# An attention block on one core: the residual x gets the projection's bias ahead of time and waits in DRAM

## The chip, the core and the metric

The kernel runs on one core of one Trainium2 chip. A core has five engines that run side by side, each through its own list of instructions in order, and wait for each other by semaphores: TensorE (PE) multiplies matrices into the accumulators (PSUM), VectorE (DVE) and ScalarE (ACT) read the accumulators and work elementwise, GpSimd (POOL) works elementwise on the on-chip memory (SBUF), and SyncE (SP) issues the DMA transfers to and from DRAM. The metric is the device time of one execution in microseconds (us), lower is better.

## The reference

A group norm, eight heads of self-attention over 2304 positions, an output projection with its bias, and the input added back; B = 4 batches, C = 512 channels, 48 x 48 positions.

```python
hn = _group_norm(x, gn_scale, gn_bias)
qkv = jnp.einsum('oc,bchw->bohw', qkv_w, hn) + qkv_b[None, :, None, None]
qkv = qkv.reshape(b, 3, num_heads, d, t).astype(jnp.float16)
q, k, v = (qkv[:, 0], qkv[:, 1], qkv[:, 2])
w = jnp.einsum('bhct,bhcs->bhts', q * scale, k * scale)
w = jax.nn.softmax(w, axis=-1)
a = jnp.einsum('bhts,bhcs->bhct', w, v).astype(jnp.float32)
out = jnp.einsum('oc,bchw->bohw', proj_w, a) + proj_b[None, :, None, None]
return x + out
```

What the change touches is the last line and the bias before it: `x + proj_b`, to which the product of the projection is added.

## The kernel before

**Tiling.** The 512 channels are four chunks of 128 partitions (`NC = 4`); the 2304 positions are five blocks (`QBLOCKS`): four of 512 columns and one of 256 (`NQ = 5`). The eight heads are four pairs per batch, so there are 16 pairs (`NG`), and of each pair 27 *bursts* (`stream`, 432 in all). The main loop (line 1544) runs over the bursts `n`. In each burst `scores` puts six matmuls into three accumulators and ACT takes their exponentials (`p`, line 1099), `add` sums the exponentials of the block on DVE (`acc`, line 1148), and `values` multiplies those of two bursts earlier by v (line 1117). After the last burst of a block come, a burst apart each: the sums (`sl`, copied to `slx`, line 1192, and sent by SP, line 1195), their reciprocal on DVE (line 1224, stored as `row` by line 1226), the reading back of the row spread over partitions (`ib`, line 1236) and the division on POOL (`att`, line 1244).

**The work beside the bursts.** Everything else that PE has to do is cut into *pieces* in the list `beside`: the chains of q and k (line 821), of v (line 873) and of the projection (line 979). `fill` gives each burst one chain, as a credit allows. All these chains use the one accumulator `pw` (`ps_w`, one buffer), so a chain can start only when DVE has emptied it of the chain before: lines 832 (`q`, `k`), 881 (`v`) and 1003 (`r`). DVE works in order, so this emptying comes behind whatever DVE has been given before it.

**The projection.** Of each batch there are 18 chains of eight matmuls (`proj_list`): for each of the four large blocks one chain for each chunk of 128 output channels, and two for the small block, of two chunks each. They run in the next batch's time: those of batches 0, 1 and 2 stand at about 630 to 760, 1040 to 1160 and 1450 to 1545 us, those of batch 3 in the last 50 us. Before a block's chains `att32` casts the heads' results to `a` on ACT (line 971) and POOL (line 969). `residual` loads the chain's part of x into a tile `r` (line 924), `add_bias` adds the bias `bproj` to it on POOL, chunk by chunk (line 935), `evacuate` adds the product from the accumulator to it on DVE (line 1003), and `store` sends it to the output (line 1006). There are `RES = NC + 2 = 6` buffers `res` for r, and `LEAD = RES - 2 = 4` loads are made ahead when block 0 begins. From then on chain k, once emptied, puts its store and the load of chain k + 4 on the list `loads`, which SP issues in the next burst. The buffers `res` also hold the four parts of the projection's weight at the start (`load_wproj`) and one block of x of batch 1 (`SPARE`).

In these same stretches the next batch is brought in: SP loads its x (line 521) when PE has done with the old block, DVE takes its statistics (line 643) and normalizes it (line 775), with one reciprocal root on POOL in between (`rstd`, line 666, which DVE takes up in line 676).

**The weight's split.** Each part of the weight is split by `split_wproj` into `whi` and `wlo` (DVE, lines 574 to 578), and POOL tests that nothing is left over (lines 579 and 580); `test_split` takes the minimum of that test on DVE (line 583). In the list `beside` it stands between the chain of k and the chain of q.

```python
for j in range(NQ):
    if j < NC:
        put_run(load_wproj, j)
    if j > 0:
        put_run(split_wproj, j - 1)
    put_qk(g + 1, 1, (j,))
    if j > 0:
        put_run(test_split, j - 1)
    put_qk(g + 1, 0, (j,))
```

Of the kernel before, what the change touches and what calls it, by code (L numbers as in the profile page):

```python
# [12 lines left out]
F32 = mybir.dt.float32  # L13
# [4 lines left out]
ALU = mybir.AluOpType  # L18
# [457 lines left out]
def fast_path(  # L476
# [11 lines left out]
):  # L488
    nc = tc.nc

    RES = NC + 2
    LEAD = RES - 2
    const = ctx.enter_context(tc.tile_pool(name="const", bufs=1))
    xpool = ctx.enter_context(tc.tile_pool(name="xpool", bufs=1))
    qkp = ctx.enter_context(tc.tile_pool(name="qkp", bufs=3))
# [281 lines left out]
    def piece(us, run, first=False, last=False, when=None):  # L777
        return [us, run, first, last, when, 0, NG]
# [129 lines left out]
    def rows_of(dram_tensor, b, j, chunks):  # L908
        o, n = QBLOCKS[j]
        found = dram_tensor[b, chunks[0] * P : (chunks[-1] + 1) * P, o : o + n]  # L910
        return found.rearrange("(m p) n -> p m n", p=P)

    def residual(b, j, chunks):
        n = QBLOCKS[j][1]
        if in_two(b, j):

            tag = f"x{chunks[0]}_{(j - NQ + 2) % 3}"
            xt = xpool.tile([P, QB], F32, tag=tag, name=f"r_{b}_{j}_{chunks[0]}")
        else:
            xt = work.tile(  # L920
                [P, QB], F32, tag="res", bufs=RES, name=f"r_{b}_{j}_{chunks[0]}"
            )
        xt = xt.rearrange("p (m n) -> p m n", n=n)
        nc.sync.dma_start(xt, rows_of(x, b, j, chunks))
        res[b, j, chunks[0]] = xt
        unbiased.append((now[0] + 2, (b, j, chunks[0]), chunks))

    unbiased = deque()

    def add_bias():  # L930
        _, key, chunks = unbiased.popleft()
        xt = res[key]
        for i, m in enumerate(chunks):
            bias = bproj[:, m : m + 1].to_broadcast((P, xt.shape[2]))
            nc.gpsimd.tensor_tensor(xt[:, i], xt[:, i], bias, ALU.add)  # L935

    def in_two(b, j):

# [50 lines left out]
    def proj_run(b, j, chunks, pairs=range(NC), bank=None):  # L989

        n = QBLOCKS[j][1]
        if bank is None:
            bank = chain_bank(f"pr_{b}_{j}_{chunks[0]}")
        places = [bank[:, i * n : (i + 1) * n] for i in range(len(chunks))]
        xt = res[b, j, chunks[0]]
        while any(k == (b, j, chunks[0]) for _, k, _ in unbiased):
            add_bias()
        for m, ps in zip(chunks, places):
            proj_chain(b, j, m, ps, pairs)

        def evacuate():
            ps = bank[:, : len(chunks) * n].rearrange("p (m n) -> p m n", n=n)
            nc.vector.scalar_tensor_tensor(xt, ps, DOWN, xt, ALU.mult, ALU.add)  # L1003

        def store(engine=nc.sync):
            engine.dma_start(rows_of(out, b, j, chunks), xt)

        return evacuate, store

    def proj_piece(b, j, chunks, pairs=range(NC), ahead=None):  # L1010
        def run():
            evacuate, store = proj_run(b, j, chunks, pairs)
            evacuate()
            if pairs == LAST:
                finished.add((j, chunks[0]))

            if pairs != FIRST:
                loads.append((now[0] + 1, store))
            if ahead is not None:
                loads.append((now[0] + 1, ahead))  # L1020

        return piece(QB / 290.0 * len(pairs) / NC, run, True, True)

    def proj_pieces(b, j):

# [277 lines left out]
    def put_qk(g, part, blocks=range(NQ)):  # L1303

        for j in blocks:
            put(qk_chain(g, part, j), (g - 2) * per_pair - 1, g)
# [39 lines left out]
    for b in range(B):  # L1346
        g = b * NPAIR
        old = b - 1
        if b == 0:
# [3 lines that stand above are left out]
                if j > 0:  # L1353
                    put_run(split_wproj, j - 1)
                put_qk(g + 1, 1, (j,))
                if j > 0:
                    put_run(test_split, j - 1)
                put_qk(g + 1, 0, (j,))
            for block in SPARE:
                put_run(reload, *block)  # L1360
        put_qk(g + 2, 1)
        put_qk(g + 2, 0)

        late = [j for j in range(NQ) if (b + 1, j) in SPARE]
        early = [j for j in range(NQ) if j not in late]
        tiles = {j: range(o // P, (o + n) // P, 2) for j, (o, n) in enumerate(QBLOCKS)}
        for j in early:
            put_v(b, 1, tiles[j])
        if b == B - 1:
            put_qk(g + 3, 1)  # L1370
            put_qk(g + 3, 0, range(NQ - 1))
            put_convert(old, 0)
            put_qk(g + 3, 0, (NQ - 1,))

            THIRD = range(len(EARLY), NC - 1)
            ahead = [
                (residual, b, j, chunks)
                for j in (NQ - 2, NQ - 3, NQ - 1)
                for jj, chunks in proj_list
                if jj == j  # L1380
            ]
            ahead += [
                (att32, b, j, (c,)) for j in (NQ - 2, NQ - 3, NQ - 1) for c in EARLY
            ]
            ahead.append((att32, b, NQ - 2, THIRD))
            for j in range(NQ):
                put_proj(old, j, ahead)
                if j + 1 < NQ:
                    put_convert(old, j + 1)
            assert not ahead  # L1390

            ahead = [
                (att32, b, NQ - 3, THIRD),
                (att32, b, NQ - 1, THIRD),
                *((att32, b, 0, (c,), True) for c in EARLY),
            ]
            for j in (NQ - 2, NQ - 3, NQ - 1):
                put_first(b, j, ahead if j != NQ - 2 else [])
            put_convert(b, 0)
            put_proj(b, 0)  # L1400
            put_convert(b, 1)
            put_proj(b, 1)
            put_convert(b, NQ - 3)
            put_proj(b, NQ - 3)
            continue

        for j in early:
            if j == NQ - 1 and b > 0:
                put_convert(old, 0)
            put_qk(g + 3, 1, (j,))  # L1410
            put_qk(g + 3, 0, (j,))
            put_run(reload, b + 1, j)
        for j in late:
            put_v(b, 1, tiles[j])
            put_qk(g + 3, 1, (j,))
            put_qk(g + 3, 0, (j,))
        if b > 0:
            for j in range(NQ - 1):
                put_proj(old, j)
                put_convert(old, j + 1)  # L1420
        put_v(b + 1, 0)
        if b > 0:
            put_proj(old, NQ - 1)
        put_qk(g + 4, 1)
        put_qk(g + 4, 0)
        put_qk(g + 5, 1)
        put_qk(g + 5, 0)
# [116 lines left out]
    for n in range(end):  # L1544
        now[0] = n
        idle_once("sync", "scalar", "gpsimd")
        summed = block_at(n - BEHIND - 1)
        if not summed:
            load_due(n)
        wanted(stream[n][0])  # L1550
        inside = n - BEHIND == soon[1]
        scores(stream[n], (lambda: values(stream[n - BEHIND])) if inside else None)
        if summed:

            rows(*summed, add_up(*summed))
            load_due(n)
        if inside:
            expect_end(kinds.DVE)
        while unbiased and unbiased[0][0] <= n:
            add_bias()  # L1560
        if n > 0:
            add(stream[n - 1])
        filled = summed or n - BEHIND - 1 in soon
        if filled:

            fill(n)
        if n >= BEHIND and not inside:
            values(stream[n - BEHIND])
        if block_at(n - BEHIND - 2):
            check_sums(*block_at(n - BEHIND - 2))  # L1570
            invert(*block_at(n - BEHIND - 2))
        if block_at(n - BEHIND - 3):
            spread(*block_at(n - BEHIND - 3))
        if block_at(n - BEHIND - 4):

            divide(*block_at(n - BEHIND - 4))
        if not filled:
            fill(n)
        while joins:
            joins.popleft()()  # L1580
        if n - BEHIND in soon:
            g, j = stream[n - BEHIND][:2]
            sx = rows(g, j, add_up(g, j))
            if n - BEHIND == soon[1]:
                divide_here(g, j, sx, avx[g, j], nc.gpsimd)
        if n - BEHIND - 1 == soon[0]:
            check_sums(g, j)
            invert(g, j)
        if n - BEHIND - 2 == soon[0]:
            spread(g, j)  # L1590
            divide(g, j)
# [143 lines left out]
```

## Time and profile before

| what | value |
|---|---|
| time of three runs | 1602.44, 1603.31, 1604.80 us (median 1603.31) |
| time of the profiled execution | 1603.71 us |
| span of its instructions | 1602.0 us |
| TensorE clock granted, mean | 0.997 |
| DMA | 82.11 MB, 51 GB/s over the span |

The span runs from the first instruction to the last; 1.7 us of the profiled execution's time lie around it. The profile's page gives the busy time of each engine; its views give who waited for whom, the instructions in order of time (start, duration, engine, line, what is written from what, how many, and in brackets the idle time of the engine before it and what ended it), and busy times by stretches of time. A matmul's end is modelled, so that the share of a busy PE tells nothing of its pace; its idle times tell where it waited.

### The profile page before, as it was taken

What the parts mean: (1) busy time and instruction counts of PE and PEld (TensorE: products, weight loads), DVE (VectorE), ACT (ScalarE), POOL (GpSimd) and SP (SyncE); (2) the same over time, 40 slices, a digit from 0 to 9 for tenths busy, and PEclk for the clock granted to TensorE, in tenths of its full rate; (3) what the DMA queues carried; (4) which work ended last, traced back from release to release, by engine and by line L of the source; (5) the groups of instructions that cost most, each with busy time, mean ns of one, the idle gap of its engine ahead of it and who ended that gap; (6) DMA issues with size and microseconds to landing.
All of it is one profiled execution on the core that took longest, in us unless ns stands there. A gap on an engine that the chain in (4) does not pass through costs nothing. (4 is left out here: it accounts for less than half of the span.)

```text
span 1602.0 us, 28595 instructions
## 1 busy us (share of the span) xinstructions
PE 1575.6 (98%) x11526; PEld 679.2 (42%) x11526; DVE 1156.8 (72%) x1302; ACT 1269.6 (79%) x1363; POOL 344.5 (22%) x305
## 2 busy tenths in 40 slices
PE   9999999999999999999999999999999999999997
PEld 3733434443333533445333354344533334434443
DVE  6277668866666678896666666898767666768786
ACT  4177777888888888788888888887878888888885
POOL 1031101101011012621101020253101110027834
PEclk9999999999999999999999999999999999999999
DMA  7002020000000024511000001352000000015423
GB/s 224 1 14 67 12 66 22 18 14 11 14 17 13 11 70 128 147 54 28 11 15 18 14 12 41 118 159 78 19 20 18 15 15 11 15 44 170 131 74 121
DMA packets 94897, 82.11 MB, mean 51 GB/s; under 512 B 50852, under 2 KB 60964, under 8 KB 94756
## 3 DMA queue, kind: packets, MB, share of 16 engines
q1 hardware_dynamic: 92724, 78.35, 17.2%
q8 instruction: 92, 1.51, 0.4%
q10 hardware_dynamic: 1904, 1.84, 0.4%
q14 instruction: 49, 0.40, 0.1%
q0 software_dynamic: 128, 0.01, 0.0%
HBM read 60.70 MB, written 19.17 MB: 50 GB/s over the span
## 5 line engine op out<-in xcount | busy, mean ns | idle before, releaser
L1099 ACT ACTIVATE p<-ps 128x1024 f16<-128x1024 f32 x1296 | 1233.2, 1025 | 301.1 <-PE ps L1092 294.1
L1148 DVE TENSOR_TENSOR acc<-acc,p 128x3072 f16<-128x3072 f16 x270 | 492.1, 1823 | 49.6 <-ACT p L1099 46.8
L821 PE MATMUL pqk<-x,wqkv 128*64 128x512 f32 (+1 forms) x2432 | 510.4, 549 | 0.7 <-DVE k L832 0.6
L1117 PE MATMUL av<-p,v 128*64 128x512 f16 (+1 forms) x2880 | 360.7, 364 | 0.9 <-DVE slx L1192 0.9
L1244 POOL TENSOR_TENSOR att<-avx,ib 128x512 f16<-128x512 f32 (+1 forms) x78 | 132.3, 1696 | 1050.0 <-DMA ib<-row 949.9
L1092 PE MATMUL ps<-q,k 64*128 64x512 f16 (+1 forms) x2880 | 356.0, 358 | 0.5 <-DVE v L881 0.2
L873 PE MATMUL pv<-wqkv,x 128*64 128x256 f32 x2304 | 267.5, 379 | 0.2 <-DVE v L881 0.2
L821 PEld LDWEIGHTS pqk<-x,wqkv 128*64 128x64 f32 x2432 | 168.7, 137 | 206.2 <-issue 155.8
L1092 PEld LDWEIGHTS <-k 64*128 64x128 f16 x2880 | 106.5, 94 | 287.6 <-issue 238.4
L1117 PEld LDWEIGHTS <-v 128*64 128x64 f16 x2880 | 131.3, 109 | 212.7 <-issue 168.0
L873 PEld LDWEIGHTS pv<-wqkv,x 128*64 128x64 f32 x2304 | 166.2, 137 | 81.3 <-DVE v L881 0.6
L1148 DVE TENSOR_TENSOR acc<-p,p 128x3072 f16<-128x3072 f16 x79 | 142.2, 1800 | 0.0
L1153 DVE TENSOR_TENSOR acc<-acc 128x1024 f16<-128x1024 f16 x156 | 120.1, 770 | 3.3
L935 POOL TENSOR_TENSOR r<-r,bproj 128x512 f32<-128x512 f32 (+1 forms) x80 | 105.2, 1336 | 33.0 <-DMA r<-x_dram 16.5
L881 DVE TENSOR_TENSOR v<-pv,bv 128x512 f16<-128x512 f32 x72 | 49.7, 690 | 81.5 <-PE pv L873 81.2
L832 DVE TENSOR_SCALAR q<-pqk,bqkv 128x512 f16<-128x512 f32 (+1 forms) x77 | 53.4, 693 | 74.6 <-PE pqk L821 74.2
L832 DVE TENSOR_SCALAR k<-pqk,bqkv 128x512 f16<-128x512 f32 (+1 forms) x75 | 52.1, 695 | 75.2 <-PE pqk L821 75.0
L979 PE MATMUL pr<-a,whi 128*128 128x512 f32 (+1 forms) x311 | 95.8, 424 | 1.9 <-POOL a L969 1.8
L1192 DVE COPY slx<-sl 128x512 f32<-128x512 f32 (+1 forms) x79 | 50.6, 641 | 62.3 <-PE sl L1176 62.2
L979 PE MATMUL pr<-att,wlo 128*128 128x512 f16 (+1 forms) x311 | 75.8, 364 | 8.8 <-DVE r L1003 8.5
L1003 DVE SCALAR_TENSOR_TENSOR r<-pr,r 128x512 f32<-128x512 f32 x75 | 51.4, 685 | 36.8 <-PE pr L979 13.9
L1126 DVE COPY avx<-av 128x512 f32<-128x512 f32 (+1 forms) x79 | 50.5, 639 | 35.7 <-PE av L1117 35.7
(125 smaller groups left out, 482.6 us busy)
## 6 DMA issues: line engine op xcount, KB each, us to landing
r<-x_dram SPq DMA_DIRECT2D x72, 256.0 KB, 3.7
out_dram<-r SPq DMA_DIRECT2D x69, 256.0 KB, 2.3
ib<-row SPq DMA_DIRECT2D x126, 128.0 KB, 2.9
x<-x_dram SPq DMA_DIRECT2D x62, 256.0 KB, 3.9
x<-x_dram SPq DMA_DIRECT2D x16, 128.0 KB, 5.0
sums<-slx SPq DMA_DIRECT2D x128, 2.0 KB, 2.1
ib<-row SPq DMA_DIRECT2D x30, 64.0 KB, 3.1
wqkv<-qkv_wT_dram SPq DMA_DIRECT2D x2, 768.0 KB, 6.9
```

The costliest lines, as they stand in the source:

```text
L821: nc.tensor.matmul(pw[0][lo : lo + D, :n], wqkv[:, c, w0 + lo : w0 + lo + D], hn[b, c, j], start=(c == 0), stop=(c == NC - 1),)
L832: nc.vector.tensor_scalar(qk[g][part][:, o : o + n], pw[0][:, :n], bqkv[:, col : col + 1], SCALE, ALU.add, ALU.mult,)
L873: nc.tensor.matmul(pw[0][lo : lo + D, a, :], hn[b, c, i * P // QB][:, at + lo : at + lo + D], wqkv[:, c, 2 * C + half * C // 2 :][:, : C / ...
L935: nc.gpsimd.tensor_tensor(xt[:, i], xt[:, i], bias, ALU.add)
L979: nc.tensor.matmul(ps[:, :n], w[:, bass.ts(m, P)], a, start=(i == 0), stop=(i == len(steps) - 1),)
L1003: nc.vector.scalar_tensor_tensor(xt, ps, DOWN, xt, ALU.mult, ALU.add)
L1092: nc.tensor.matmul(ps[:, h, a * n : (a + 1) * n], kt[rows, bass.ts(i, P)], qt[rows, o : o + n], start=True, stop=True,)
L1099: nc.scalar.activation(pt[:, r], ps, AF.Exp)
L1117: nc.tensor.matmul(av[0][lo : lo + D, :n], vv[b, pr // 2][:, i, pr % 2 * P + lo : pr % 2 * P + lo + D], pt[:, r, h, a * n : (a + 1) * n], ...
L1148: nc.vector.tensor_tensor(t, before, pt, ALU.add)
L1153: nc.vector.tensor_tensor(t[:, 0], t[:, 0], t[:, r], ALU.add)
L1244: nc.gpsimd.tensor_tensor(atts[g][:, o : o + n], avx.pop((g, j))[:, :n], ibs.pop((g, j))[:, :n], ALU.mult,)
```

## The change

`residual` no longer loads x but a tile `xb` in DRAM that holds x plus the bias already. These 72 tiles are made by three new steps in earlier bursts: `fetch_x` loads a part of x into a buffer `pre` (two of them; SP), `add_bias` adds the bias two bursts later in one instruction (POOL; before, the small block took two), and `keep_biased` stores it to `xb` a burst after that (SP). `prepare` calls the first and the last at the start of a burst. It makes no fetch before burst 30, none within two bursts of another, none in the bursts in which the `row` or `ib` transfers of a block are due, and none while a chain of the projection is among the next four pieces. The two buffers come from `res`: `RES` is 4 now and `LEAD` is 2, so a residual is loaded when the chain two places before it has been emptied. The wait of a chain for its bias goes. `test_split` stands behind the chain of q now, so one chain later, and for the last part behind the first chain of the next pair.

```diff
-    RES = NC + 2
+    RES = NC
     LEAD = RES - 2
+    FETCH_FROM, FETCH_EVERY = 30, 2
...
-        nc.sync.dma_start(xt, rows_of(x, b, j, chunks))
+        nc.sync.dma_start(xt, biased.pop((b, j, chunks[0])))
         res[b, j, chunks[0]] = xt
-        unbiased.append((now[0] + 2, (b, j, chunks[0]), chunks))
-
-    unbiased = deque()
+
+
+    biased, heavy = {}, set()
+    to_bias = deque((b, j, chunks) for b in range(B) for j, chunks in proj_list)
+    fetched, added = deque(), deque()
+
+    def fetch_x():
+        b, j, chunks = to_bias.popleft()
+        n = QBLOCKS[j][1]
+        name = f"{b}_{j}_{chunks[0]}"
+        t = work.tile([P, QB], F32, tag="pre", bufs=2, name=f"pre_{name}")
+        t = t.rearrange("p (m n) -> p m n", n=n)
+        nc.sync.dma_start(t, rows_of(x, b, j, chunks))
+        fetched.append((now[0] + 2, (b, j, chunks), t))
 
     def add_bias():
-        _, key, chunks = unbiased.popleft()
-        xt = res[key]
-        for i, m in enumerate(chunks):
-            bias = bproj[:, m : m + 1].to_broadcast((P, xt.shape[2]))
-            nc.gpsimd.tensor_tensor(xt[:, i], xt[:, i], bias, ALU.add)
+        _, key, t = fetched.popleft()
+        chunks = key[2]
+        bias = bproj[:, chunks[0] : chunks[-1] + 1].unsqueeze(2)
+        nc.gpsimd.tensor_tensor(t, t, bias.to_broadcast(t.shape), ALU.add)
+        added.append((now[0] + 1, key, t))
+
+    def keep_biased():
+        _, (b, j, chunks), t = added.popleft()
+        name = f"xb_{b}_{j}_{chunks[0]}"
+        kept = dram.tile(list(t.shape), F32, tag=name, bufs=1, name=name)
+        nc.sync.dma_start(kept, t)
+        biased[b, j, chunks[0]] = kept
+
+    fetch_at = [FETCH_FROM]
+
+    def prepare(n):
+        if added and added[0][0] <= n:
+            keep_biased()
+        transfers = block_at(n - BEHIND - 2) or block_at(n - BEHIND - 3)
+        if any(id(p) in heavy for p in beside[:4]):
+            fetch_at[0] = max(fetch_at[0], n + 2)
+        elif to_bias and n >= fetch_at[0] and not transfers:
+            fetch_x()
+            fetch_at[0] = n + FETCH_EVERY
...
-        while any(k == (b, j, chunks[0]) for _, k, _ in unbiased):
-            add_bias()
...
-        return piece(QB / 290.0 * len(pairs) / NC, run, True, True)
+        made = piece(QB / 290.0 * len(pairs) / NC, run, True, True)
+        heavy.add(id(made))
+        return made
...
                 put_qk(g + 1, 1, (j,))
-                if j > 0:
+                put_qk(g + 1, 0, (j,))
+                if 0 < j < NC:
                     put_run(test_split, j - 1)
-                put_qk(g + 1, 0, (j,))
+            put_qk(g + 2, 1, (0,))
+            put_run(test_split, NC - 1)
...
-        put_qk(g + 2, 1)
+        put_qk(g + 2, 1, range(0 if b else 1, NQ))
...
             load_due(n)
+            prepare(n)
...
-        while unbiased and unbiased[0][0] <= n:
+        if fetched and fetched[0][0] <= n and not block_at(n - BEHIND - 4):
             add_bias()
```

On PE and on ACT the order of all instructions stays as it was. Three places show what moves on the others. Names end in a block number, a chunk number and a serial number; the changed kernel's lines from `add_bias` on stand 31 lower than before (1275 is the division of 1244, 667 the root of 666).

**POOL, in the projection of batch 0.** Before, from the division of block 3 of the pair to that of block 4:

```order
L1244 TENSOR_TENSOR att_5605<-avx_3_6405,ib_3_6560 128x512
L935 TENSOR_TENSOR r_2_1_6530<-r_2_1_6530,bproj 128x512
L1217 TENSOR_SCALAR in_4_6655<-sums_170 128x40
L1218 TENSOR_TENSOR tests<-tests,in_4_6655 128x40
L1217 TENSOR_SCALAR in_4_6658<-sums_170 128x40
L1218 TENSOR_TENSOR tests<-tests,in_4_6658 128x40
L935 TENSOR_TENSOR r_2_2_6598<-r_2_2_6598,bproj 128x512
L666 TENSOR_TENSOR rstd<-veps,mhalf 128x2
L935 TENSOR_TENSOR r_2_3_6632<-r_2_3_6632,bproj 128x512
L1244 TENSOR_TENSOR att_5605<-avx_4_6558,ib_4_6703 128x256
```

And the same place in the changed kernel:

```order
L1275 TENSOR_TENSOR att_5765<-avx_3_6586,ib_3_6738 128x512
L1248 TENSOR_SCALAR in_4_6831<-sums_170 128x40
L1249 TENSOR_TENSOR tests<-tests,in_4_6831 128x40
L1248 TENSOR_SCALAR in_4_6834<-sums_170 128x40
L1249 TENSOR_TENSOR tests<-tests,in_4_6834 128x40
L667 TENSOR_TENSOR rstd<-veps,mhalf 128x2
L1275 TENSOR_TENSOR att_5765<-avx_4_6736,ib_4_6878 128x256
```

The three bias additions that stood here are gone; they stand between divisions outside the projections.

**SP, as the projection of batch 1 begins.** Before, from the spread rows of block 4 on:

```order
L1236 DMA ib_4_10439<-row_4_10398 64x256 x2
L1006 DMA out_dram<-r_0_0_10306 128x512
L924 DMA r_1_0_10454<-x_dram 128x512
L1006 DMA out_dram<-r_0_1_10308 128x512
L924 DMA r_1_1_10490<-x_dram 128x512
L1006 DMA out_dram<-r_0_2_10310 128x512
L924 DMA r_1_2_10525<-x_dram 128x512
```

And the same place in the changed kernel:

```order
L1267 DMA ib_4_10741<-row_4_10700 64x256 x2
L1035 DMA out_dram<-r_0_0_10616 128x512
L925 DMA r_0_2_10756<-xb_0_2_4502 128x512
L1035 DMA out_dram<-r_0_1_10618 128x512
L925 DMA r_0_3_10792<-xb_0_3_4534 128x512
L1035 DMA out_dram<-r_0_2_10756 128x512
L925 DMA r_1_0_10827<-xb_1_0_4711 128x512
```

Behind the store of chain 0 the load of chain 2 is issued now, and no longer that of chain 4; it reads `xb`.

**DVE, at the last part of the weight's split** (the burst in which the sums of block 1 are copied to `slx`). Before:

```order
L1126 COPY avx_1_1189<-av_1_1000 128x512
L832 TENSOR_SCALAR k_699<-pqk_1_4_1191,bqkv 128x256
L583 TENSOR_REDUCE tests<-wproj_1043 128x1
L1192 COPY slx_1_1229<-sl_1_1226 128x512
L1148 TENSOR_TENSOR acc_2_1233<-p_2_0_1131,p_2_1_1170 128x3072
```

And the same place in the changed kernel, up to where the test stands now:

```order
L1157 COPY avx_1_1189<-av_1_999 128x512
L833 TENSOR_SCALAR k_699<-pqk_1_4_1191,bqkv 128x256
L1223 COPY slx_1_1228<-sl_1_1225 128x512
L1179 TENSOR_TENSOR acc_2_1232<-p_2_0_1130,p_2_1_1170 128x3072
L833 TENSOR_SCALAR q_698<-pqk_0_4_1234,bqkv 128x256
L1179 TENSOR_TENSOR acc_2_1232<-acc_2_1232,p_2_2_1212 128x3072
L1255 RECIPROCAL inv_1_1282<-sums_168 128x8
L833 TENSOR_SCALAR k_1287<-pqk_1_0_1288,bqkv 128x512
L584 TENSOR_REDUCE tests<-wproj_1043 128x1
```

The test (583, now 584) has moved from ahead of the copy of the sums to six instructions behind it.

## The prediction

> **What bounds the kernel now.** I read the busy times of the page first, then what PE waited for, then the stretches in which it waited.
>
> ```profile
> PE 1575.6 (98%) x11526; PEld 679.2 (42%) x11526; DVE 1156.8 (72%) x1302; ACT 1269.6 (79%) x1363; POOL 344.5 (22%) x305
> PE pr L979 <- DVE r L1003: 8.5, 9, 2.7
> PE pr L979 <- POOL a L969: 1.8, 3, 0.7
> PE av L1117 <- DVE slx L1192: 0.9, 1, 0.9
> PE pqk L821 <- DVE k L832: 0.6, 2, 0.4
> PE count L1674 <- DVE good L1673: 2.5, 1, 2.5
> ```
>
> PE is busy for 1575.6 of 1602.0 us, so all its idle time is 26.4 us. The change gives PE the same instructions in the same order, so it can win only idle time and lost clock. The rows of the waits give total, times and longest. 8.5 us are waits of a projection chain for the emptying of the accumulator, 1.8 for a cast on POOL, 0.9 for the copy of the sums, 0.6 for k; together 11.8. The 2.5 us for `good` belong to the end, which the change does not touch.
>
> ```profile
> 200.00:400.00 200.00, 199.90 (x1556) 85.71 (x1552) 151.06 (x180) 161.27 (x171) 21.88 (x19) 1.00 0.11 26
> 600.00:760.00 160.00, 156.19 (x1178) 74.37 (x1176) 135.24 (x166) 130.72 (x143) 49.19 (x43) 0.99 0.31 90
> 1000.00:1140.00 140.00, 136.67 (x1016) 63.06 (x1014) 122.54 (x154) 115.40 (x129) 53.77 (x45) 1.00 0.35 104
> 1420.00:1560.00 140.00, 136.25 (x882) 61.11 (x880) 108.37 (x106) 120.44 (x136) 79.41 (x64) 1.00 0.39 115
> 673.85:677.25 3.40, 3.40 (x10) 1.78 (x11) 2.30 (x2) 1.07 (x2) 0.18 (x1) 0.54 0.48 151
> ```
>
> These are windows: stretch, length, busy time of PE, weight load, DVE, ACT and POOL, granted clock, DMA share, GB/s. Between projections PE loses 0.1 us in 200. In the three projections it loses 3.8, 3.3 and 3.8; there POOL is two to five times as busy. The last row is the 3.4 us behind the longest wait: the clock is 0.54, which costs 3.4 x 0.46 = 1.6 us more.
>
> **The split test.**
>
> ```profile
> 126.39 0.69 DVE L583 TENSOR_REDUCE tests<-wproj 128x1 f32<-128x512 f32 x1 [1.63 <-POOL wproj L580]
> 127.73 0.84 PE L1117 MATMUL av<-p,v 128*64 128x512 f16 x6 [0.94 <-DVE slx L1192]
> ```
>
> The last test keeps DVE waiting 1.63 us for POOL; behind it stands the copy of the sums, and PE waits 0.94 for that. Moved six instructions back, the test finds its input made. **Gain 0.9**, between 0.2 (the next chain late instead) and 1.2 (with the 0.25 left of the k waits).
>
> **Batch 0.**
>
> ```profile
> 624.77 2.57 DVE L1148 TENSOR_TENSOR acc<-p,p 128x3072 f16<-128x3072 f16 x1
> 628.38 1.95 PE L821 MATMUL pqk<-x,wqkv 128*64 128x256 f32 x16 [0.36 <-DVE k L832]
> 642.81 1.02 PE L979 MATMUL pr<-att,wlo 128*128 128x512 f16 x4 [0.46 <-DVE r L1003]
> 666.48 1.04 POOL L935 TENSOR_TENSOR r<-r,bproj 128x512 f32<-128x512 f32 x1
> 667.48 2.24 POOL L666 TENSOR_TENSOR rstd<-veps,mhalf 128x2 f32<-128x2 f32 x1
> 669.75 1.01 DVE L676 COPY both<-rstd 128x32 f32<-128x32 f32 x1 [0.62 <-POOL rstd L666]
> 673.85 1.86 PE L979 MATMUL pr<-att,wlo 128*128 128x512 f16 x4 [2.68 <-DVE r L1003]
> ```
>
> The longest wait is a chain of queues: a bias addition, behind it on POOL the root `rstd`, behind that on DVE line 676 and the emptying. Without the addition the root starts up to 1.04 us earlier, and DVE has no 0.62 to wait; the normalization behind it runs beside no addition either. I take the 2.68 as gone, with the 1.6 of clock, the 0.36 at 628.38 and a smaller 0.17: **gain 4.8**. The 0.46 at 642.81 stands beside a division and stays. If only 1.04 of the 2.68 goes, and half the clock, it is 2.3; all of it is 5.3.
>
> By the Trainium skill (TensorE: Matmul & The Clock Gate, What's actually happening) the clock falls after at least one idle window of about 3.4 us. This wait was 2.68 and the clock fell right behind it; by the page the 1.6 would not hang on the wait, and the sum would come out 1.6 higher. I go by the row.
>
> **Batch 1.**
>
> ```profile
> 1076.05 2.57 DVE L1148 TENSOR_TENSOR acc<-p,p 128x3072 f16<-128x3072 f16 x1
> 1080.25 1.02 PE L979 MATMUL pr<-att,wlo 128*128 128x512 f16 x4 [0.65 <-DVE r L1003]
> 1084.94 2.44 DVE L775 TENSOR_SCALAR x<-x,ga,gb 128x512 f32<-128x512 f32 x2
> 1088.03 1.02 PE L979 MATMUL pr<-att,wlo 128*128 128x512 f16 x4 [0.88 <-DVE r L1003]
> 1092.89 1.02 PE L979 MATMUL pr<-att,wlo 128*128 128x512 f16 x4 [1.38 <-DVE r L1003]
> 1043.48 0.67 DVE L1003 SCALAR_TENSOR_TENSOR r<-pr,r 128x512 f32<-128x512 f32 x1
> 1046.34 0.42 SPq L924 DMA_DIRECT2D r<-x_dram  x1
> 1050.33 0.68 DVE L1003 SCALAR_TENSOR_TENSOR r<-pr,r 128x512 f32<-128x512 f32 x1
> 1051.43 1.07 POOL L935 TENSOR_TENSOR r<-r,bproj 128x512 f32<-128x512 f32 x1 [1.57 <-DMA r<-x_dram]
> ```
>
> The three waits make 2.91; sums and normalizations stretched beside POOL stand ahead of each. Divisions remain, so I take 2.2 (0 to 2.9). Against it stands the shorter lead: the place after the first store, 1046.34, now loads chain 2, which is emptied at 1050.33. That load, of the same size, was taken up at 1051.43, so chain 2 would be 1.1 late. **Gain 1.1**, between -1.1 and 2.9.
>
> **Batches 2 and 3.**
>
> ```profile
> 1481.41 1.06 PE L979 MATMUL pr<-a,whi 128*128 128x512 f32 x2 [0.54 <-POOL a L969]
> 1487.87 1.02 PE L979 MATMUL pr<-att,wlo 128*128 128x512 f16 x4 [0.43 <-DVE r L1003]
> 1551.85 7.12 POOL L935 TENSOR_TENSOR r<-r,bproj 128x512 f32<-128x512 f32 x4 [9.61 <-DMA r<-x_dram]
> 1553.67 1.02 PE L979 MATMUL pr<-att,wlo 128*128 128x512 f16 x4 [1.41 <-DVE r L1003]
> 1578.44 0.38 PE L979 MATMUL pr<-att,wlo 128*128 128x512 f16 x1 [0.42 <-DVE r L1003]
> ```
>
> In batch 2 the casts stand behind additions on POOL: 1.8 and 0.43, of which I take **2.0** (1.0 to 2.2). In batch 3 the first addition waits for its load and takes a us itself; now two loads are sent instead of four and nothing is added. Of 1.41 + 0.42 I take **1.7** (0.5 to 1.8).
>
> **What the quiet stretches take over.** 72 additions come into them.
>
> ```profile
> 606.28 1.75 DVE L1148 TENSOR_TENSOR acc<-acc,p 128x3072 f16<-128x3072 f16 x1
> L935 POOL TENSOR_TENSOR r<-r,bproj 128x512 f32<-128x512 f32 (+1 forms) x80 | 105.2, 1336 | 33.0 <-DMA r<-x_dram 16.5
> L1244 POOL TENSOR_TENSOR att<-avx,ib 128x512 f16<-128x512 f32 (+1 forms) x78 | 132.3, 1696 | 1050.0 <-DMA ib<-row 949.9
> ```
>
> 105 us of POOL move. In the window 200 to 400, 21.88 us of POOL cost PE at most 0.10; 105 us cost at that rate **0.5**. The other end: a sum beside an addition took 2.57 instead of 1.75, so 0 to 0.82 an addition; at half of it, 0.41, all reaching PE, 72 cost 29.5. I take 0.5, since in that window DVE has a quarter of its time free. What waits newly: each `keep_biased` holds SP until POOL has added, which may stand behind a division; behind it on SP are the sums, rows and spread rows of later blocks, and behind these the divisions. A division waits for its `ib` 949.9/78 = 12 us on the mean already and PE asks for none before the projection: nothing, up to 2 us if that cover fails. The 144 added transfers of 256 KB are 37.7 MB, over some 1000 us 38 GB/s beside 26, which takes the DMA share from 0.11 to about 0.27, below that of the projections: nothing.
>
> The Trainium skill (SBUF — State Buffer, Who interferes with whom) says that a DVE instruction with two SBUF inputs contends with a GpSimd instruction that reads SBUF. The 2.57 agrees; were every addition to hold up a sum for its whole 1.04 us, and PE with it, the sum would be 72 x 1.04 = 75 us worse, which the window speaks against.
>
> **Next late.** With the additions gone DVE is still 85% busy there beside divisions, and some chain is late behind it: **-1.0** (0 to -3).
>
> The sum: 0.9 + 4.8 + 1.1 + 2.0 + 1.7 - 0.5 - 1.0 = 9.0. From the profiled 1603.71 this gives 1594.7; the median is 0.4 lower than that execution, so 1594.3, and I say **1594.5**. All gains at their upper ends make 13.4 (1590), half the sum, 4.5 to 5, 1598.5: its own range. All lower ends together would use the gain up; that they fall together is what the rivals are.
>
> **The rivals.**
>
> *The loads take the wait over.* Loads two places ahead have two bursts: 1043.48 to 1050.33, 6.85 us.
>
> ```profile
> DMA to landing us min/median/max: 2.0/3.0/5.7
> 1562.56 0.69 DVE L1003 SCALAR_TENSOR_TENSOR r<-pr,r 128x512 f32<-128x512 f32 x1 [0.75 <-POOL r L935]
> 1565.08 0.58 SPq L1006 DMA_DIRECT2D out_dram<-r  x1
> ```
>
> The store comes 2.5 us after the emptying where sums are sent ahead of it, the load 0.7 later; with 3.0 to land that is 6.2, still in time, with 5.7 it is 8.9, 2 us late. If 12 of the 72 chains are 0.5 late, 6 us go: 1600.5.
>
> *The bias was not the cause.* Batch 1's three waits stay (2.2 lost) and the next-late term is 3.0 instead of 1.0: gain 4.8, 1598.5. For it: divisions are as many and longer, 1.70 us each. Against it: the longest wait and the casts stand directly behind additions.
>
> *The clock falls anyway*, wait or no wait: 1.6 less gain, 1596.1.
>
> *Slower: the additions stretch DVE in the quiet stretches and PE waits there.* From 9.5/72 = 0.13 us of PE for each addition the gain is used up; at 0.41 it is 1603.7 - 9.5 + 29.5, about 1623. For it: the 2.57. Against it: the window 200 to 400, whose ten-odd us of divisions cost nothing visible.
>
> **How the numbers follow.** Forecast 0.62, loads 0.16, bias not the cause 0.08, clock 0.05, slower 0.09. A measurement of this kernel can tell about 0.2%, 3.2 us, from no change: faster is below 1600.1, slower above 1606.5. Faster: nearly all of the forecast (0.60), the clock (0.05), most of the third (0.06), a third of the loads (0.05), 0.76. Within: the rest of these, 0.14. Slower: 0.10. The range goes from 1589.5, all gains, to 1602, past the loads' 1600.5; what is left out is the slower case and the loads' far end.
>
> **What would show it.** Right: the wait of 2.68 and the 0.54 clock are gone, no PE wait for the copy of the sums near 127, none for the casts, and quiet windows stay above 99.9% PE. Wrong: an emptying that waits for a residual's load (first chain 2 of batch 1), PE idle in quiet stretches behind sums longer than 1.75, or POOL waiting for a `pre` buffer with divisions behind it.

## The result, and the profile after

| what | before | changed |
|---|---|---|
| median of the runs | 1603.59 us (4 runs) | 1592.71 us (4 runs) |
| span of the profiled execution | 1602.0 us | 1591.4 us |
| PE busy | 1575.6 us | 1573.6 us |
| PE idle within the span | 26.4 us | 17.8 us |

The ratio is 0.9933, with a 95% interval of 0.9915 to 0.9950. The forecast was 1594.5, with a range of 1589.5 to 1602. The span is 10.6 us shorter. PE's idle time makes 8.6 of it and its busy time, in which a lower clock shows, 2.0.

First what PE waited for in the changed kernel (total, times, longest, in us), from the view of its waits:

```profile
PE pr L1010 <- DVE r L1032: 1.1, 2, 0.8
PE pv L874 <- DVE v L882: 1.0, 2, 0.9
PE pqk L822 <- DVE v L882: 0.9, 1, 0.9
PE pqk L822 <- DVE k L833: 0.9, 2, 0.6
PE sl L1207 <- DVE avx L1157: 0.8, 2, 0.6
PE first_means L722 <- DVE moments L648: 0.6, 1, 0.6
PE pr L1010 <- POOL a L1000: 0.6, 1, 0.6
```

Of the 8.5 us of waits for an emptied projection accumulator 1.1 are left, of the 1.8 for casts 0.6. Four rows are new or larger: the two of v, k and `avx`, 3.6 us together, against 0.8 before. The wait for `first_means`, at the start of the kernel, was 1.3 before; it lay between under 0.2 and 1.4 in the profiles of this study, also where nothing ahead of it was changed, so its 0.7 us here are no effect of the change.

The same windows of the changed kernel (stretch, length, busy time of PE, weight load, DVE, ACT, POOL, granted clock, DMA share, GB/s):

```profile
200.00:400.00 200.00, 198.17 (x1542) 84.91 (x1540) 157.61 (x179) 159.72 (x169) 46.18 (x35) 1.00 0.24 68
600.00:760.00 160.00, 159.36 (x1212) 75.09 (x1210) 137.23 (x170) 134.54 (x148) 40.59 (x36) 1.00 0.40 121
673.85:677.25 3.40, 3.40 (x21) 1.53 (x20) 3.37 (x5) 3.40 (x6) 2.17 (x3) 1.00 0.61 203
1000.00:1140.00 140.00, 138.76 (x1042) 64.66 (x1038) 121.36 (x154) 117.68 (x130) 28.74 (x29) 1.00 0.42 123
1420.00:1560.00 140.00, 139.10 (x897) 63.54 (x894) 104.62 (x109) 124.48 (x141) 29.20 (x33) 1.00 0.41 121
```

The projections lose 0.6, 1.2 and 0.9 us where they lost 3.8, 3.3 and 3.8, and the clock behind 673 is 1.00. The quiet window 200 to 400 now loses 1.8 instead of 0.1: part of the gain is given back there. Two places of the timeline show how (start, duration, engine, line, operation, what ended the idle time before it):

```profile
273.70 1.04 POOL L946 TENSOR_TENSOR pre<-pre,bproj 128x512 f32<-128x512 f32 x1
273.79 2.57 DVE L1179 TENSOR_TENSOR acc<-p,p 128x3072 f16<-128x3072 f16 x1
277.98 1.94 PE L822 MATMUL pqk<-x,wqkv 128*64 128x512 f32 x8 [0.93 <-DVE v L882]
605.40 1.04 POOL L946 TENSOR_TENSOR pre<-pre,bproj 128x512 f32<-128x512 f32 x1 [2.60 <-DMA pre<-x_dram]
605.49 2.57 DVE L1179 TENSOR_TENSOR acc<-p,p 128x3072 f16<-128x3072 f16 x1
609.37 1.94 PE L822 MATMUL pqk<-x,wqkv 128*64 128x512 f32 x8 [0.64 <-DVE k L833]
```

An addition meets a sum, the sum takes 2.57 instead of 1.75, and the emptying behind it is late for PE. Near 323 the same happens, with 0.87. And the load that comes two places ahead is late once, as batch 1's projection begins:

```profile
1043.68 0.42 SPq L925 DMA_DIRECT2D r<-xb  x1
1048.39 0.69 DVE L1032 SCALAR_TENSOR_TENSOR r<-pr,r 128x512 f32<-128x512 f32 x1 [1.42 <-PE av L1148]
1049.14 1.02 PE L1010 MATMUL pr<-att,wlo 128*128 128x512 f16 x4 [0.80 <-DVE r L1032]
```

The load landed at 1047.93, 4.25 us after its issue, and DVE, which had nothing else to do, empties then. The `av` named in brackets is not what it waited for: the chain to be emptied was complete at 1046.82.

### The profile page after: what moved, and what is told of

Read it like the earlier page. It is cut to its first block, busy times and chain, and to the rows that moved or that the text cites. A ratio compares the mean times of both kernels' runs of the same rounds, so it can differ in the third digit from the quotient of the medians.

```text
span 1591.4 us, 28818 instructions
## 1 busy us (share of the span) xinstructions
PE 1573.6 (99%) x11526; PEld 678.2 (43%) x11526; DVE 1171.2 (74%) x1302; ACT 1269.0 (80%) x1363; POOL 337.0 (21%) x297
## 5 line engine op out<-in xcount | busy, mean ns | idle before, releaser
L1275 POOL TENSOR_TENSOR att<-avx,ib 128x512 f16<-128x512 f32 (+1 forms) x78 | 117.3, 1504 | 1009.0 <-DMA ib<-row 674.7
L1184 DVE TENSOR_TENSOR acc<-acc 128x1024 f16<-128x1024 f16 x156 | 136.4, 874 | 3.3
L946 POOL TENSOR_TENSOR pre<-pre,bproj 128x512 f32<-128x512 f32 x72 | 115.1, 1613 | 22.3 <-DMA pre<-x_dram 21.7
```

The lines of the kernel that those rows point to most:

```text
L946: nc.gpsimd.tensor_tensor(t, t, bias.to_broadcast(t.shape), ALU.add)
L1184: nc.vector.tensor_tensor(t[:, 0], t[:, 0], t[:, r], ALU.add)
L1275: nc.gpsimd.tensor_tensor(atts[g][:, o : o + n], avx.pop((g, j))[:, :n], ibs.pop((g, j))[:, :n], ALU.mult,)
```

## The experiments

The times stand beside runs of the kernel before on the same chip; the experiments ran in three groups, on three chips. The kernel before took 1603.83 beside experiments 1, 2, 3 and 5; 1603.92 beside 6, 7, 9 and the first run of 8; 1603.24 beside 4, 10 and the second run of 8.

**1. No additions at all.** In the kernel before, the three lines that add are left out:

```diff
-        for i, m in enumerate(chunks):
-            bias = bproj[:, m : m + 1].to_broadcast((P, xt.shape[2]))
-            nc.gpsimd.tensor_tensor(xt[:, i], xt[:, i], bias, ALU.add)
```

> The kernel before with the additions of the bias left out (the bias is not added). If PE's waits in the projections come from the additions on POOL (theory): the waits of a projection chain for an emptying or a cast fall from 10.3 us to under 2.5, the clock behind 673 stays at 1.0, about 11 us less, 1592. If they come from DVE's own load and the divisions (rival): under 5 us less, 1598 or more, and the waits of 2.7 and 1.4 stay over 1 us.

Measured: 1589.95 (ratio 0.9908, 0.9893 to 0.9924). A window of this kernel:

```profile
600.00:760.00 160.00, 160.00 (x1216) 75.31 (x1214) 133.79 (x169) 135.43 (x149) 28.33 (x27) 1.00 0.32 91
```

The projection of batch 0 now loses nothing, although all divisions still run there. So the 80 additions cost 13.9 us in their old places. Three waits of 2.4 us together remain before projection chains (1.33, 0.62 and 0.43); the 1.33 stands behind a reciprocal on DVE that waited 2.43 for the transfer of its sums, so not behind a division. The theory stands; the rival falls.

**2. The changed kernel without its additions.** The addition of `add_bias` is left out; fetches and stores to `xb` stay.

```diff
-        bias = bproj[:, chunks[0] : chunks[-1] + 1].unsqueeze(2)
-        nc.gpsimd.tensor_tensor(t, t, bias.to_broadcast(t.shape), ALU.add)
```

> The changed kernel with the additions left out (the bias is not added), all its transfers kept. If the new waits of PE near 278, 323 and 609 us (0.9, 0.9 and 0.6) come from the additions in the quiet stretches (theory): they go, 2.3 us less, 1590.4. If they come from the 144 transfers or from the moved test (rival): they stay, within 0.5 us of the changed kernel.

Measured: 1589.27 (0.9903, 0.9888 to 0.9918), 3.4 under the changed kernel's 1592.71 and 2.4 under the 1591.66 that the same kernel took in experiment 8; each of the three was measured in another group of runs. The window from 130 to 600, in the changed kernel first and then here:

```profile
130.00:600.00 470.00, 468.17 (x3550) 194.26 (x3546) 350.27 (x366) 378.11 (x398) 106.97 (x79) 1.00 0.23 65
```

```profile
130.00:600.00 470.00, 469.89 (x3566) 195.30 (x3564) 335.55 (x369) 379.94 (x400) 50.54 (x46) 1.00 0.23 67
```

The DMA share is the same and PE's 1.8 us of idle time fall to 0.1. The additions make the waits, the transfers none. The late load as batch 1 begins stays, here with a wait of 1.25.

**3. Only the shorter lead.** The kernel before with four buffers, its additions in place.

```diff
-    RES = NC + 2
+    RES = NC
```

> The kernel before with four buffers for the residuals and loads two places ahead; its additions stay in the projections. If the shorter lead costs only the one late load at the start of a batch (theory): 1 to 2 us more, 1604.5 to 1605.5, with a wait of about 2 near 1050 (load plus addition). If the loads as a whole become late (rival): over 6 us more, and waits for the residual in each batch.

Measured: 1619.91 (1.0093, 1.0077 to 1.0108), 16 us more. The theory was wrong by a factor of ten. The rows of PE's and DVE's waits, and the timeline in batch 0:

```profile
PE pr L979 <- DVE r L1003: 26.8, 22, 3.0
DVE r L1003 <- POOL r L935: 40.5, 25, 4.1
...
661.01 0.42 SPq L924 DMA_DIRECT2D r<-x_dram  x1
669.71 0.72 POOL L666 TENSOR_TENSOR rstd<-veps,mhalf 128x2 f32<-128x2 f32 x1 [3.52 <-DVE both L669]
670.40 1.04 POOL L935 TENSOR_TENSOR r<-r,bproj 128x512 f32<-128x512 f32 x1
671.48 0.69 DVE L1003 SCALAR_TENSOR_TENSOR r<-pr,r 128x512 f32<-128x512 f32 x1 [1.76 <-POOL r L935]
672.22 1.02 PE L979 MATMUL pr<-att,wlo 128*128 128x512 f16 x4 [1.77 <-DVE r L1003]
```

DVE's emptyings wait 40.5 us for additions, where they waited 10.5 in the kernel before. In the place shown the load is not late: it landed at 663.93, 2.9 us after its issue. Its addition comes two bursts after the load, which is now just ahead of the emptying, and on POOL it stands behind the root; DVE can empty only when it is done. In other places the addition starts as its load lands. So whether the loads or what stands behind them makes the 16 us was open; experiment 4 settles it.

**4. Only the shorter lead, no additions.** Both edits above together.

> The kernel before with four buffers, loads two places ahead and no additions (the bias is not added). The 16 us of the shorter lead with additions come either from a load that needs an addition behind it before the chain can be emptied (theory): then the shorter lead alone costs 0 to 2 us, 1590 to 1592. Or from the loads landing late (rival): then 1600 and more.

Measured: 1589.23 (0.9911, 0.9896 to 0.9927).

```profile
600.00:760.00 160.00, 160.00 (x1216) 75.25 (x1213) 134.53 (x170) 135.44 (x149) 25.85 (x27) 1.00 0.32 91
```

Without additions the lead of two costs nothing (1589.95 with the lead of four). The load alone is in time, but for the one in the changed kernel as batch 1 begins; a load with an addition behind it is not. So the shorter lead and the earlier bias belong together: the first alone is 16 us slower.

**5. One addition moved.** Of the kernel before, the addition for chain (2, 2) of batch 0 is due a burst later, which puts it behind the root; no other instruction changes its order.

```diff
-        unbiased.append((now[0] + 2, (b, j, chunks[0]), chunks))
+        wait = 3 if (b, j, chunks[0]) == (0, 2, 2) else 2
+        unbiased.append((now[0] + wait, (b, j, chunks[0]), chunks))
```

> The kernel before with one of the 80 additions, the one ahead of the reciprocal root in batch 0, moved behind that root; nothing else. If the longest wait is the queue on POOL and the clock falls because PE stood still (theory): the wait of 2.68 falls under 1.2 and the clock stays at 1.0, 3 to 4.3 us less, about 1599.8. If DVE's load makes it (rival): the wait falls by less than 0.5 us and the time by less than 1. If the clock falls for another reason: the wait is short, the clock at 673 to 677 still about 0.54.

Measured: 1602.4 (0.9992, 0.9983 to 1.0001). The timeline and the clock of the 3.4 us behind the wait:

```profile
666.33 0.72 POOL L666 TENSOR_TENSOR rstd<-veps,mhalf 128x2 f32<-128x2 f32 x1
668.45 1.02 DVE L676 COPY both<-rstd 128x32 f32<-128x32 f32 x1
672.57 1.02 PE L980 MATMUL pr<-att,wlo 128*128 128x512 f16 x4 [1.54 <-DVE r L1004]
679.84 1.02 PE L980 MATMUL pr<-att,wlo 128*128 128x512 f16 x4 [0.62 <-DVE r L1004]
```

```profile
672.57:675.97 3.40, 3.40 (x20) 1.51 (x19) 3.37 (x3) 2.26 (x5) 1.84 (x4) 1.00 0.48 155
```

The wait falls from 2.68 to 1.54, half way between the two theories, and a new one of 0.62 comes behind it. The clock stays at 1.00 behind it. What is left of the wait comes from the steps of DVE between root and emptying, which run beside the moved addition now. The copy of line 676 takes 1.02 here; in the changed kernel, with no addition near, it takes 0.17:

```profile
667.75 0.72 POOL L667 TENSOR_TENSOR rstd<-veps,mhalf 128x2 f32<-128x2 f32 x1 [0.62 <-DVE both L670]
669.95 0.17 DVE L677 COPY both<-rstd 128x32 f32<-128x32 f32 x1
```

So without the queue on POOL 1.1 of the 2.7 are gone, and what is left goes with stretched steps; experiment 7 shows the same from the other side. Here the change wins 0.5 of net idle time and the 1.6 of clock. The times of all runs show 1.4, less than the 3 to 4.3 of the theory, and their interval does not exclude no change.

**6. The move of the test alone,** in the kernel before.

> The kernel before with the move of the test alone. If the wait only changes its place (theory, from the changed kernel's trace): the 0.94 near 128 goes, waits of 0.58 and 0.24 for the copy of av near 103 and 125 come, 0.1 us less. If the move is worth its wait (rival, as predicted): 0.9 us less. The time cannot tell these apart, the waits of PE below 130 us can.

Measured: 1603.34 (0.9998, 0.9988 to 1.0007). Its waits at the two places:

```profile
103.03 0.41 PE L1176 MATMUL sl<-acc,ones 128*64 128x512 f16 x2 [0.58 <-DVE avx L1126]
125.22 0.41 PE L1176 MATMUL sl<-acc,ones 128*64 128x512 f16 x2 [0.24 <-DVE avx L1126]
```

They are the changed kernel's own, to the hundredth. The 0.94 near 128 is gone and 0.82 stand in its place: the test's 0.67 us now stand between q and the next part's split, and the copy of `av` behind them is late. By these waits the move is worth 0.1.

**7. Additions of a tensor and a scalar.** The bias is one number for each partition, so the addition need not read two tensors. In the kernel before (its places kept):

```diff
-            bias = bproj[:, m : m + 1].to_broadcast((P, xt.shape[2]))
-            nc.gpsimd.tensor_tensor(xt[:, i], xt[:, i], bias, ALU.add)
+            nc.gpsimd.tensor_scalar(
+                xt[:, i], xt[:, i], bproj[:, m : m + 1], None, ALU.add
+            )
```

> The kernel before, the additions where they were, but as an operation of a tensor and a scalar of each partition instead of two tensors. If an addition disturbs DVE because it reads two tensors (theory): sums beside it take under 2 us, the waits in the projections fall from 10.3 to under 6, 4 us less or more, 1599. If any POOL work beside DVE disturbs it (rival): waits as before, within 1 us.

Measured: 1605.26 (1.0006, 0.9997 to 1.0015).

```profile
624.54 1.75 DVE L1149 TENSOR_TENSOR acc<-p,p 128x3072 f16<-128x3072 f16 x1
667.58 0.18 DVE L676 COPY both<-rstd 128x32 f32<-128x32 f32 x1 [0.61 <-POOL rstd L666]
670.04 1.02 PE L980 MATMUL pr<-att,wlo 128*128 128x512 f16 x4 [0.64 <-DVE r L1004]
PE pr L980 <- POOL a L970: 5.5, 4, 2.0
PE pr L980 <- DVE r L1004: 5.1, 5, 2.2
```

The sum that took 2.57 beside an addition takes 1.75, and the wait of 2.68 falls to 0.64. The root still stands behind an addition on POOL there, and DVE still waits 0.61 for it; but the copy of line 676 takes 0.18. So of the 2.68 some 0.6 to 1.1 are the queue (this experiment and experiment 5), and the larger part is stretched steps of DVE. But POOL now pays: the addition's mean rises from 1336 to 1867 ns, and casts behind seven and eight of them in a row make PE wait 5.5 us instead of 1.8. The theory stands for the sum, but the waits it wanted under 6 are 10.6, and the time is no better.

**8. The same in the changed kernel,** where no cast stands behind the additions. It ran twice, the second time beside the changed kernel.

> The changed kernel with the additions as tensor and scalar of each partition. By the first theory (two tensors disturb): the waits of 0.9, 0.9 and 0.6 near 278, 323 and 609 shrink, 1 to 2.5 us less than the changed kernel, about 1591. By the rival: 1592.7, the waits stay.

> The changed kernel once more, beside the three others: about 1592.7, with the same new waits near 278, 323, 609 and 1049 us.

> The changed kernel with scalar additions once more. If they help (theory): 1 to 2.5 us under the changed kernel of this call. If the difference of the first time was chance (rival): within 0.7 us of it.

Measured: 1591.13 the first time; the second time 1589.03 (five runs, 1588.68 to 1590.09) beside the changed kernel's 1591.66 (five runs, 1590.49 to 1592.85). The place of before, in the second profile:

```profile
273.38 3.16 POOL L946 TENSOR_SCALAR pre<-pre,bproj 128x512 f32<-128x512 f32 x1
273.44 1.75 DVE L1181 TENSOR_TENSOR acc<-p,p 128x3072 f16<-128x3072 f16 x1
277.22 1.94 PE L822 MATMUL pqk<-x,wqkv 128*64 128x512 f32 x8 [0.52 <-DVE v L882]
```

The addition started first, by 0.06 us, and is still the one that is held up (3.16), where the one of two tensors held up DVE. The wait of 0.93 falls to 0.52, and that of 0.87 goes. The 0.64 near 609 proves nothing: the changed kernel's own second profile does not have it either, since there the addition began 0.87 us ahead of the sum and the sum took 1.78. That profile has the 0.93 and the 0.87 again, and the late load with 0.49. So the theory stands; the gain is 1.6 us across two groups and 2.6 side by side.

**9. Every addition twice.**

```diff
-        nc.gpsimd.tensor_tensor(t, t, bias.to_broadcast(t.shape), ALU.add)
+        for _ in range(2):
+            nc.gpsimd.tensor_tensor(t, t, bias.to_broadcast(t.shape), ALU.add)
```

> The changed kernel with every addition made twice in a row (the bias is counted twice). If a quiet addition costs PE what leaving them out showed (theory, 3.4 us for 72, 0.05 each): 2 to 5 us more, 1595 to 1598. If DVE has little free time left and the next additions all reach PE (rival, 0.41 each): 20 us more or above, 1612.

Measured: 1593.78 (0.9935, 0.9922 to 0.9949), 1.1 over the changed kernel's 1592.71 and 2.1 over its 1591.66, so at the lower edge of the theory or under it, and far from the rival. The longest new wait, of 0.93, grows to 1.77. But DVE is busy 17.7 us longer in the profile and PE idle only 2.0: most of the added time falls where DVE has time to spare. What an addition costs depends more on where it lands than on how many there are.

**10. Scalar additions, and the tests a chain later still.** Behind the next chain of k instead of between q and the next split:

```diff
                 put_qk(g + 1, 1, (j,))
+                if 1 < j:
+                    put_run(test_split, j - 2)
                 put_qk(g + 1, 0, (j,))
-                if 0 < j < NC:
-                    put_run(test_split, j - 1)
```

> The changed kernel with scalar additions, and each test of the split another chain later, behind the next chain of k. If the waits of 0.58 and 0.24 near 103 and 125 come from the test standing between q and the next split (theory): they go, 0.5 to 0.8 us less than with scalar additions alone. If any place there costs the same DVE time (rival): they come back in front of another instruction, no gain.

Measured: 1587.50 (0.9903, 0.9888 to 0.9918; four runs, 1587.37 to 1588.21). Below 130 us one of the waits remains, which all kernels have:

```profile
102.96 1.97 PE L822 MATMUL pqk<-x,wqkv 128*64 128x512 f32 x8 [0.25 <-DVE k L833]
```

The 0.58 and the 0.24 are gone, the 0.94 does not come back. The time is 1.5 under experiment 8's 1589.03, more than the expected 0.5 to 0.8 and than the 0.82 of these waits; the rest has no row of its own. This kernel leaves nothing out and is the fastest of all: 4.2 us under the changed kernel beside it, with no overlap of their runs.

## Why the prediction was right

The time was 1.8 us under the forecast. What gains and what costs was as forecast, with errors in size on both sides that nearly cancel, which is in part luck. Measured by the waits of PE that went and came, in the first profile of the changed kernel:

| term | predicted | measured | from |
|---|---|---|---|
| split test | 0.9 | 0.1 | 0.94 gone, 0.58 and 0.24 come |
| batch 0, with the clock | 4.8 | 5.4 | 0.36, 0.11, 0.46, 0.17, 2.68 gone, clock 1.6 |
| batch 1 | 1.1 | 2.2 | 3.0 gone, late load 0.80 |
| batch 2 | 2.0 | 1.6 | 2.2 gone, one cast late by 0.62 |
| batch 3 | 1.7 | 1.6 | 1.83 gone, 0.28 come |
| quiet additions | -0.5 | -2.3 | 0.93 (0.1 before), 0.87, 0.64 come |
| next late | -1.0 | 0 | the new 0.62 and 0.28 stand with their batches |

The measured rows make 8.6 of the 10.6. A second reading needs no waits: how much earlier the same exponential of ACT (line 1099, now 1130; 1296 of each) starts. It gives:

| stretch, up to exponential | its start in the kernel before, us | gained in the stretch, us |
|---|---|---|
| start, 1 | 73.25 | -0.2 |
| split test, 52 | 137.13 | 0.3 |
| quiet, 456 | 610.61 | -3.0 |
| batch 0, 521 | 692.66 | 5.8 |
| quiet, 821 | 1037.22 | -0.2 |
| batch 1, 881 | 1111.25 | 2.3 |
| quiet, 1181 | 1450.98 | 0.0 |
| batch 2, 1234 | 1517.16 | 3.2 |
| batch 3, 1296 | 1584.91 | 1.4 |
| end of the span | 1602.0 | 1.0 |

The shorter wait at the start gains nothing. Batch 2 gains twice what its waits say. So the four batches gained 12.7 where the prediction, with next late, had 8.6, and the split test and the quiet stretches lost 2.9 where it had a gain of 0.4.

Of its signs of being right, the 2.68 and the clock of 0.54 are gone and PE has no wait for the copy of the sums; but one cast is late by 0.62, and the quiet window has 99.1% of PE and not 99.9%. Two signs of being wrong came, both small: the late load of batch 1, and waits behind sums of 2.57.

**Batch 0** was right in its parts: the wait, the queue ahead of it and the clock went together. Experiments 5 and 7 show that the queue ("the root starts up to 1.04 us earlier") is less than half of it and that the stretched steps of DVE are the rest, so taking the whole 2.68 was right only because all additions leave. The clock at 1.00 behind the shorter wait, and where the wait is gone, bears out that the 1.6 hung on the wait. (Where the prediction says "the sum would come out 1.6 higher", it is the time that would; the gain would be 1.6 smaller, as its rival of the clock has it.) That it would be lost with every such wait was not asked and is not so (last section).

**Batch 1** was too low by 1.1. All three waits went, although the divisions stayed ("divisions remain, so I take 2.2"): experiment 1 shows that divisions alone do not make them. The late first load came where the prediction put it, 0.80 for 1.1 (0.49 in the second profile).

**Batch 2** was too low, 2.0 for 3.2 by the second reading. The waits named in the prediction went; that they cost more time than their rows say was not foreseen, and why is not shown.

**The split test** was mis-sized, 0.9 for 0.1 by its waits and 0.3 by the second reading. "Moved six instructions back, the test finds its input made" is true of the last test; the prediction did not ask what the earlier tests, moved too, now stand ahead of.

**The quiet additions** were mis-sized most: 0.5 for 2.3 by the waits and 3.0 by the second reading (2.1 in the second profile, which lacks the 0.64). The 0.5 was a rate from divisions in a quiet window, and an addition of two tensors that starts just ahead of a sum disturbs it more. Leaving them out gives 2.4 to 3.4. The bounds had held it (0 to 29.5); the slower rival, 0.41 for each, fell with experiment 9, where 72 more cost 1.1 to 2.1.

**Next late** came, if the new waits of 0.62 and 0.28 are counted here and not with batches 2 and 3: 0.9 for 1.0. The rival of the loads fell in the changed kernel, since a lead of two suffices without additions; experiment 3 shows how near it stood, for the same lead with additions costs 16 us. The forecast had not seen that the two edits need each other.

## What to carry to other kernels

Work off the critical path still sets the pace when it stands, in an in-order queue, ahead of a small step that the critical engine waits for, or when it slows such a step beside it; look for the stretched neighbours of a wait as well as for the queue. A step between a load and its use makes the buffer's lead longer by its whole queue, so taking it out can pay for fewer buffers. When something is moved out of the way, ask for each of its instances what it now stands ahead of.

## What was not expected of the hardware

- Between an addition on POOL and a sum on DVE the order decides who gives way, and the operands how long. An addition of two tensors that started 0.09 us ahead of a sum kept its 1.04 us, and the sum took 2.57 instead of 1.75 (273.70 and 273.79 in the changed kernel). Where the sum started 0.09 ahead, it kept its time and the addition took 2.56:

```profile
858.75 1.76 DVE L1179 TENSOR_TENSOR acc<-acc,p 128x3072 f16<-128x3072 f16 x1 [0.78 <-ACT p L1130]
858.84 2.56 POOL L946 TENSOR_TENSOR pre<-pre,bproj 128x512 f32<-128x512 f32 x1
```

  In the kernel before, 15 sums started less than 0.9 us into an addition that kept its time; each ended 2.65 to 2.66 us after the addition's start, so as if held until 0.9 us into it. Beside additions of a tensor and a scalar (experiment 7, and the second run of 8) nine sums that started 0.2 to 0.5 us into one ended 2.29 to 2.30 after its start, as if held until 0.55; where nothing else held the addition up, sums that started between 0.58 and 1.5 into one took their 1.75 and the addition its 1.56 to 1.73. So the sums are held up less by these, and more of the waiting falls to POOL. Experiment 8's 3.16, of an addition that began 0.06 ahead of its sum and still gave way, does not fit the order in the rows; why is not shown.
- The length of a wait alone does not decide whether the clock falls. Behind the waits of 2.02 us before 1470.92 and of 2.97 us before 1496.67 in experiment 3 it fell the first time and not the second:

```profile
1470.92 1.44 PE L979 MATMUL pr<-att,wlo 128*128 128x512 f16 x3 [2.02 <-DVE r L1003]
1496.67 1.02 PE L979 MATMUL pr<-att,wlo 128*128 128x512 f16 x4 [2.97 <-DVE r L1003]
```

```profile
1467.48:1470.89 3.41, 1.42 (x12) 0.45 (x9) 0.72 (x2) 2.85 (x3) 3.02 (x3) 1.00 0.51 192
1470.89:1474.30 3.41, 3.38 (x8) 1.74 (x7) 3.27 (x2) 1.05 (x2) 2.86 (x3) 0.50 0.72 231
1491.37:1494.79 3.42, 2.32 (x22) 1.16 (x21) 0.77 (x1) 3.01 (x4) 2.82 (x2) 1.00 0.89 288
1494.79:1498.20 3.41, 1.53 (x7) 1.04 (x7) 2.28 (x2) 1.10 (x2) 3.41 (x5) 1.00 0.32 113
1498.20:1501.61 3.41, 2.81 (x25) 1.33 (x24) 3.38 (x5) 2.62 (x3) 3.41 (x4) 1.00 0.31 84
```

  The clock stands at 0.50 for one stretch of 3.41 us, here from 1470.89. Counted on in steps of 3.41, the 2.02 lies in one stretch, and the 2.97 is cut in two by the border at 1494.79. The study's five falls before the end of a kernel all fit: each comes behind a stretch in which PE was busy for 0.94 to 1.60 us of 3.41, with a wait of 1.81 to 2.79 for the most part in it (of the 2.68 of the kernel before, 2.36). The waits of 2.51 in experiment 3 and 2.18 in experiment 7, which cost no clock, were cut by a border too. How little busy time it takes is not shown: the 1.53 of the stretch from 1494.79 was followed by no fall.

  The Trainium skill (TensorE: Matmul & The Clock Gate, What's actually happening) has windows of about 3.4 us that run freely, which would let equal waits end differently; that the clock falls behind waits well under one window, as here, its rule of an idle window does not say. The traces agree with the windows that run freely, and not with the need for an idle one.

- Tiny steps of DVE are stretched too: the copy of 128 x 32 took 1.01 to 1.02 us beside an addition and 0.17 without.
